# Two spectral layers rewritten around two passes over image planes held with the images innermost

## The chip, the core and the metric

The kernel runs on one core of a Trainium2 chip: PE (TensorE) for matrix products into PSUM banks of 512 float32 columns, DVE (VectorE), ACT (ScalarE) and POOL (GpSimd) for elementwise work, SP and ACT as the issuers of DMAs. The metric is the device time of one execution in microseconds (us). Everything is float32, and each float32 product shows in the trace as two records of PE, each with its weight load; a transpose shows as one.

## The reference

Two layers of the same form act on x of shape (2, 56, 128, 128): two batches of 56 images, 128 by 128. Cut to what matters, one layer is:

```python
def spectral_conv(x, w, b):          # 32 x 16 Fourier modes are kept
    xf = jnp.fft.rfft2(x, norm='forward')
    top = jnp.einsum('bihw,iohw->bohw', xf[:, :, :M1, :M2], _c(w[0]))
    bot = jnp.einsum('bihw,iohw->bohw', xf[:, :, -M1:, :M2], _c(w[1]))
    ...
    return jnp.fft.irfft2(of, s=(H, W), norm='forward') + b

def fno_layer(x, w, b, sw, sb, norm=False, act=False):
    y = spectral_conv(x, w, b)
    if norm: y = inorm(y)
    y = y + skip1x1(x, sw, sb)
    return jax.nn.gelu(y, approximate=False) if act else y

xn = inorm(xa, g1, b1)               # xa: the 112 images
k, q, v = (fno_layer(xn, ...) for each, 8 heads)
scores = jnp.einsum('baks,bals->bakl', qh, kh) * scale
out = softmax(scores) @ v            # mixes the 56 images of a batch
out = fno_layer(out, Pw, Pb, Psw, Psb)
att = inorm(out + xa, gan, ban)
an = inorm(att, g2, b2)
h = fno_layer(an, M0w, ..., norm=True, act=True)
h = fno_layer(h, M1w, ..., norm=True, act=False)
y = inorm(h, gmo, bmo) + att
```

Twice, with weights of their own, `x = x + layer(_gn(x))`, where `_gn` is a group norm over the images of a batch, all h and groups of four w; it has no gain and no offset.

## The kernel before

The planes stand in SBUF as `X` and `A`, each [h, image, w]: 128 partitions of h, 112 images, 128 w. A layer goes over them stage by stage, and each stage goes over all images before the next begins.

- Group norm, then instance norm, for each batch: sums of `X` by products with ones (L340), squares and their sums (L352, L353), the scaling (L364), `bn_stats` of every image row (L326), and the instance norm in place (L376, L378). So the planes are gone over four times on DVE.
- `to_rows` (L270) and `to_modes` (L282, L289) take the planes to 32 x 16 modes, held as `xf` and, with real and imaginary parts exchanged, `xs`. The products of all pairs of images (the Gram matrix) are taken one w at a time (L394), with `A[:, images, w]`, whose elements stand 512 bytes apart, as both operands.
- The scores come from the modes (L386 to L406) and the Gram matrix; softmax; then `D`, the attention applied on the modes (L453 to L455).
- The mix: four w at a time, PE transposes `A` (L462), ACT copies the result to SBUF (L464), PE multiplies with `mix` (L467), and the result goes back into `A`.
- `from_modes` takes modes back to planes: eight small DMAs to memory and two back, a rearrangement on POOL (L308), products L312 and L319. It is used three times in a layer, each with its own finish on DVE: `add_out` (L474, L326), `act` (L542, and ACT's gelu, L545), `skip` (L557, L326). Between these, `to_rows` and `to_modes` are done twice more, and `normed` scales the coefficients.
- The final norm and the sum with the residual (L578 to L582); in the last layer the output DMAs.

The framework places the instructions: the program's order is a first order, and a scheduler moves instructions of each engine within it. The engines then work strictly in the placed order, and tiles of rotating pools set when a buffer comes free.

Of the kernel before, what the change touches and what calls it, by code (L numbers as in the profile page):

```python
# [47 lines left out]
def _constants():  # L48
# [13 lines left out]
    swap[p, p ^ 16] = 1
    row = 8 * (p // 32)[:, None] + np.arange(8)
    edge = kx[:, None] == 0
    sgn = np.where(c == 0, -1.0, 1.0)[:, None]
    own = np.where(edge, 0.5, np.ones((N, 8)))
    mirror = np.where(edge & (row != 16), 0.5, np.zeros((N, 8)))
    count = np.where(edge & (row != 16), 1.0, np.full((N, 8), 2.0))
    count0 = np.where(edge & (row == 0), 0.0, count)
    modes = np.stack([own, mirror, -mirror, count, count * sgn, count0, sgn + np.zeros((N, 8))], 1)  # L70
    place = np.zeros((K, 3 * K))
    place[:, K : 2 * K] = np.eye(K)
# [567 lines left out]
```

## Time and profile before

| what | us |
|---|---|
| three timed runs | 1414.13, 1415.04, 1426.47 |
| their median | 1415.04 |
| profiled execution, span from its first to its last instruction | 1412.7 |
| PE busy in it | 1003.7 |
| DVE busy in it | 819.8 |
| ACT busy in it | 306.0 |
| POOL busy in it | 211.9 |
| mean granted clock of PE | 0.747 |

The span is the only time that is recorded of the profiled execution; the timed runs are other executions. [...] Busy shares are averages over stages that differ, so that a stage is read by its own rows.

### The profile page before, as it was taken

To read this page: it belongs to the slowest core of one execution; us is meant where nothing else is said; L and a number is where in the kernel's file an instruction comes from. 1 tells how busy PE (TensorE), PEld (TensorE's weight loads), DVE (VectorE), ACT (ScalarE), POOL (GpSimd) and SP (SyncE) were. 2 spreads that over 40 slices of the span, in tenths; PEclk is the share of its full clock that TensorE was granted. 3 is DMA by queue.
4 is the path that set the end of the run, shared out by engine and by line. 5 is a ranking of instruction groups with operands and counts; after the bars stand their busy time and mean duration, and the time that the engine had idled before them with its cause. 6 is when DMAs were issued, how large, how long until landed. Compare 5 with 4: busy or idle time off the path is not lost.

```text
span 1412.7 us, 13545 instructions
## 1 busy us (share of the span) xinstructions
PE 1003.7 (71%) x4992; PEld 695.5 (49%) x4992; DVE 819.8 (58%) x2052; ACT 306.0 (22%) x536; POOL 211.9 (15%) x259
## 2 busy tenths in 40 slices
PE   5374899798778936948633849989877887287550
PEld 1151788346664823724212438944566556146320
DVE  2367452791116797528978581739411397873498
ACT  0222200002221203410352321010122112152024
POOL 6603040000001013011131110400000001301102
PEclk9777599665558977979866957986555599599685
DMA  9000000001000010010000000000100000100106
GB/s 260 0 1 1 0 1 1 1 0 26 0 1 1 1 27 0 1 27 1 1 0 1 0 0 1 1 0 0 26 0 1 0 1 0 27 1 1 26 16 193
DMA packets 38872, 22.89 MB, mean 16 GB/s; under 512 B 8606, under 2 KB 37654, under 8 KB 38806
## 3 DMA queue, kind: packets, MB, share of 16 engines
q1 hardware_dynamic: 37216, 20.19, 5.8%
q10 hardware_dynamic: 1590, 1.83, 0.5%
q8 instruction: 39, 0.64, 0.2%
q14 instruction: 27, 0.22, 0.1%
HBM read 11.93 MB, written 10.09 MB: 16 GB/s over the span
## 4 chain that ended last, share of the span: by engine, by line
PE 60%; DVE 22%; ACT 8%; issue 3%; DMA 3%; POOL 3%; SPq 1%; ACTq 0%; POOLq 0%; DVEq 0%
PE mm L270 12%; PE acc L394 9%; PE mm L467 9%; PE mm L319 9%; DVE rows L326 6%; PE mm L453 5%; PE acc L353 3%; PE mm L312 3%; ACT t L464 3%; DVE A L364 2%; DVE A L580 2%; DVE A L557 2%; PE mm L462 2%; PE acc L340 2%; ACT A L128 2%
## 5 line engine op out<-in xcount | busy, mean ns | idle before, releaser
L319 PE MATMUL mm<-c_gw,t 128*128 128x512 f32 x336 | 168.8, 646 | 31.1 <-ACT t L316 31.1
L270 PEld LDWEIGHTS mm<-c_fh,A 128*128 128x128 f32 x1344 | 168.7, 206 | 8.5 <-issue 3.9
L270 PE MATMUL mm<-c_fh,A 128*128 128x64 f32 x1344 | 172.8, 291 | 0.0
L467 PE MATMUL mm<-mixT,t 112*128 112x112 f32 x512 | 131.2, 438 | 46.5 <-ACT t L464 46.5
L467 PEld LDWEIGHTS mm<-mixT,t 112*128 112x128 f32 x512 | 114.1, 328 | 72.8 <-ACT t L464 72.8
L308 POOL COPY lc<-spec 64x128 f32<-64x128 f32 x84 | 52.7, 655 | 627.7 <-PE mm L312 339.0
L126 DVE COPY A<-mm 128x448 f32<-128x448 f32 x32 | 29.1, 908 | 188.2 <-PE mm L467 188.2
L326 DVE BATCH_NORM_STATS2 rows<-A 128x6 f32<-128x128 f32 x672 | 137.0, 275 | 0.1
L394 PE MATMUL acc<-A 128*56 128x56 f32 x1024 | 134.0, 312 | 0.0
L394 PEld LDWEIGHTS acc<-A 128*56 128x56 f32 x1024 | 128.6, 226 | 6.1 <-issue 3.2
L319 PEld LDWEIGHTS mm<-c_gw,t 128*128 128x128 f32 x336 | 65.2, 205 | 108.1 <-issue 52.9
L126 DVE COPY big<-mm 128x512 f32<-128x512 f32 (+1 forms) x50 | 48.2, 971 | 98.6 <-PE mm L270 98.2
L312 PE MATMUL mm<-c_gh,lc 64*64 64x128 f32 x672 | 51.1, 297 | 75.0 <-POOL lc L308 75.0
L128 ACT COPY big<-mm 128x512 f32<-128x512 f32 (+1 forms) x50 | 47.8, 956 | 204.5 <-PE mm L270 138.9
L312 PEld LDWEIGHTS mm<-c_gh,lc 64*64 64x64 f32 x672 | 40.0, 145 | 104.0 <-POOL lc L308 76.1
L353 PE MATMUL acc<-t,ones_gn 128*128 128x512 f32 x112 | 57.1, 665 | 47.6 <-ACT t L352 47.6
L453 PE MATMUL mm<-attnT,big 56*128 56x448 f32 x128 | 82.8, 822 | 3.7 <-DVE spec L454 3.6
L542 DVE SCALAR_TENSOR_TENSOR A<-A,s,mm 128x128 f32<-128x128 f32 x224 | 59.4, 341 | 28.3 <-PE mm L319 28.3
L316 ACT COPY t<-mm 128x512 f32<-128x512 f32 x42 | 24.6, 586 | 220.6 <-PE mm L312 220.6
L462 PE MATMUL mm<-c_ident,A 128*112 128x128 f32 x256 | 68.0, 421 | 0.0
L340 PE MATMUL acc<-X,ones_gn 128*128 128x512 f32 x112 | 60.4, 688 | 10.1 <-DMA X<-x 7.6
L464 ACT COPY t<-mm 112x512 f32<-112x512 f32 x64 | 37.5, 586 | 136.5 <-PE mm L462 136.5
(170 smaller groups left out, 1239.9 us busy)
## 6 DMA issues: line engine op xcount, KB each, us to landing
X<-x SPq DMA_DIRECT2D x14, 512.0 KB, 7.3
out<-X SPq DMA_DIRECT2D x28, 256.0 KB, 2.3
turned<-spec SPq DMA_DIRECT2D x48, 56.0 KB, 2.0
spec<-turned SPq DMA_DIRECT2D x12, 224.0 KB, 3.7
raw<-weights ACTq DMA_DIRECT2D x2, 544.0 KB, 5.0
c_gw<-const_gw ACTq DMA_DIRECT2D x1, 256.0 KB, 5.3
sm<-small ACTq DMA_DIRECT2D x2, 63.0 KB, 5.5
c_swap<-const_swap ACTq DMA_DIRECT2D x1, 64.0 KB, 5.7
```

The source lines that it names most:

```text
L126: nc.vector.tensor_copy(to, of)
L270: nc.tensor.matmul(py[:, 64 * e : 64 * e + 64], lhsT=A[:, i + e, :], rhs=fh, start=True, stop=True)
L312: nc.tensor.matmul(pz[64 * c : 64 * c + 64, N * e : N * e + N], lhsT=four, rhs=gh[:, c, :], start=True, stop=True,)
L319: nc.tensor.matmul(po, lhsT=z[:, N * e : N * e + N], rhs=gw, start=True, stop=True)
L326: nc.vector.bn_stats(rows[:, k, :], A[:, i, :])
L340: nc.tensor.matmul(acc, lhsT=ones_gn, rhs=X[:, i : i + 4, :], start=(i == lo), stop=(i + 4 == hi))
L353: nc.tensor.matmul(acc2, lhsT=ones_gn, rhs=sq, start=(i == lo), stop=(i + 4 == hi))
L394: nc.tensor.matmul(acc[:K, :K], lhsT=plane, rhs=plane, start=(w == 0), stop=(w == N - 1))
L453: nc.tensor.matmul(pv, lhsT=XT[:, b, n, t, :], rhs=aT[b], start=True, stop=True)
L462: nc.tensor.transpose(pt[:I, N * e : N * e + N], A[:, :, w + e], ident)
L464: nc.scalar.copy(xt[:I, :], pt[:I, :])
L467: nc.tensor.matmul(po[:, I * e : I * e + I], lhsT=xt[:I, N * e : N * e + N], rhs=mix, start=True, stop=True)
```

## The change

One layer is written anew. In the code of after:

- The planes stand as `XI` [image, h, w]: 120 partitions, batch 0 in 0 to 55, batch 1 in 64 to 119, zeros between (L164, L165). For the sums over w they are transposed once in a layer into `T` [w, h, image] (L388), with `bn_stats` over the images of four rows at a time (L391), which gives the group norm's mean and variance by a product with `four` (L397, L405).
- `T` is normed in place (L418), and `to_rows` (L304) now takes the sum over w for 16 rows of h, in four products of 32 weight columns, and sends the result by way of memory to `U` [h, mode, image]. The Gram matrix is summed one h at a time, with 64 and 56 weight columns into two halves of one bank (L422). The mean and variance of each image come from the Gram matrix and the modes, so that the instance norm is not applied to the planes at all.
- Scores, softmax and `D` are as before in kind, for both batches in one tile of 120 partitions (L466 to L575).
- The variances that `att`, `an`, M0 and M1 need come from modes, the Gram matrix and the mix `m2` (L585 to L601, L689 to L694), not from planes.
- Pass 1 (L662 to L675) and pass 2 (L722 to L738) are the only two passes over planes after that. `inverse` sums in one bank the modes' contribution (L366, weights of 32 partitions) and the mix of the images (L371, weights from `XI`). Pass 1 applies gelu to it and goes on to the next transform (L304) and the energy of h (L674, L675). Pass 2 scales and adds h (L726 on POOL, L731 on DVE), transposes back (L736) and adds into `XI` (L738). `to_columns` (L341, L352) and `columns` (L357) carry the modes by way of memory to these passes, 480 bytes at a time.
- `prepare` gathers a layer's multipliers in `packed` and reorders them by a product on PE (L272), two copies on ACT and eleven DMAs on SP (L279, L282).

At the head of the program, PE's rows of before and of after (in after `packed` is what POOL makes of the weights; `mm` and `acc` are banks of PSUM, `t2` the squares of `X`, and a number behind a name tells one tile of it from another):

```order
L340 MATMUL acc_202<-X_93,ones_gn_109 128x512 x14
L353 MATMUL acc_221<-t2_223,ones_gn_109 128x512
L353 MATMUL acc_221<-t2_227,ones_gn_109 128x512
L353 MATMUL acc_221<-t2_231,ones_gn_109 128x512
L353 MATMUL acc_221<-t2_235,ones_gn_109 128x512
```

```order
L272 MATMUL mm_219<-c_order_126,packed_178 128x128 [waits DMAHW5_49,Pool_49]
L272 MATMUL mm_219<-c_order_126,packed_178 128x128 [waits Pool_49]
L272 MATMUL mm_219<-c_order_126,packed_178 64x128
L388 MATMUL mm_241<-c_ident_118,XI_93 128x120 [waits DMAHW3_49,DMAHW1_49,DMAHW0_49]
L388 MATMUL mm_241<-c_ident_118,XI_93 128x120 x3
L388 MATMUL mm_249<-c_ident_118,XI_93 128x120 x4
```

The three reordering products, which wait for POOL, now stand ahead of the transposes of the input planes; in before nothing of `prepare` stands on PE.

Where the Gram matrix and the first transform run beside each other, PE's rows of before and of after:

```order
L394 MATMUL acc_846<-A_94 56x56 x16
L270 MATMUL mm_716<-c_fh_121,A_94 128x64 x8
L394 MATMUL acc_846<-A_94 56x56
L270 MATMUL mm_726<-c_fh_121,A_94 128x64 x3
L394 MATMUL acc_846<-A_94 56x56
L270 MATMUL mm_726<-c_fh_121,A_94 128x64 x2
```

```order
L422 MATMUL sums_516<-big_239 64x56
L304 MATMUL mm_519<-big_239,c_fw_122 32x480 x4
L304 MATMUL mm_530<-big_239,c_fw_122 32x480 x4
L422 MATMUL sums_516<-big_239 56x56
L422 MATMUL sums_516<-big_239 64x56
L304 MATMUL mm_541<-big_239,c_fw_122 32x480 x4
L422 MATMUL sums_516<-big_239 56x56
```

In after a Gram product has 64 or 56 weight columns and writes one or the other half of the bank `sums`; `to_rows` has gone from 64 columns for each image to four products of 480.

In the mix of before, and in pass 2 of after, with what each row waits for (`DVE_49` and the like are semaphores):

```order
L462 MATMUL mm_1365<-c_ident_127,A_94 112x128 [waits DVE_49]
L462 MATMUL mm_1365<-c_ident_127,A_94 112x128 x3
L467 MATMUL mm_1372<-mixT_1183,t2_1370 128x112 [waits Activation_49]
L467 MATMUL mm_1372<-mixT_1183,t2_1370 128x112 x3
L462 MATMUL mm_1378<-c_ident_127,A_94 112x128 [waits DVE_49]
L462 MATMUL mm_1378<-c_ident_127,A_94 112x128 x3
L467 MATMUL mm_1385<-mixT_1183,t2_1383 128x112 [waits DVE_49,Activation_49]
L467 MATMUL mm_1385<-mixT_1183,t2_1383 128x112 x3
```

```order
L366 MATMUL mm_1893<-z_1842,basis_894 128x4x56 x2
L371 MATMUL mm_1893<-mixer_1805,XI_93 128x120 x4
L736 MATMUL mm_1902<-c_ident_118,tmp1_160 120x128 [waits DVE_49,PE_49]
L736 MATMUL mm_1902<-c_ident_118,tmp1_160 120x128 x3
L366 MATMUL mm_1911<-z_1908,basis_894 128x4x56 [waits DMAHW4_49,PE_49]
L366 MATMUL mm_1911<-z_1908,basis_894 128x4x56
L371 MATMUL mm_1911<-mixer_1805,XI_93 128x120 x4
L736 MATMUL mm_1920<-c_ident_118,tmp0_158 120x128 [waits DVE_49,PE_49]
```

In both, PE's row of products is followed by one that waits for the engine that takes those products out of PSUM; in after that is the transposes L736 behind L371, with the products of the next quarter behind them.

The diff, cut to its core:

```diff
+        pk = bank()
+        for n in range(3):
+            c = packed[:, 16 * n : min(16 * n + 16, 40), :].rearrange("p n t -> p (n t)")
+            nc.tensor.matmul(pk[: c.shape[1], N * n : N * n + N], lhsT=c, rhs=order, start=True, stop=True)
+        kept = wp.tile([N, 3, N], F32, name="kept")
+        nc.scalar.copy(kept[:, 0:2, :].rearrange("p n m -> p (n m)"), pk[:, 0 : 2 * N])
+        nc.scalar.copy(kept[:64, 2, :], pk[:64, 2 * N : 3 * N])
+        wt = dram.tile([40, 8, N], F32, name="wt")
+        for n in range(3):
+            to = wt[16 * n : min(16 * n + 16, 40)].rearrange("n t m -> (n t) m")
+            nc.sync.dma_start(out=to, in_=kept[: to.shape[0], n, :])
+        mult = wq.tile([N, 40, 8], F32, name="mult")
+        for t in range(8):
+            nc.sync.dma_start(out=mult[t::8], in_=wt[:, t, :].rearrange("n (x s) -> x n s", s=8))
...
-    def to_modes(Y):
+    def to_rows(T, g, turned, U):
+        pv = bank()
+        for q in range(4):
+            nc.tensor.matmul(pv[32 * q : 32 * q + 32, : 4 * J], lhsT=fw, rhs=quarter(T, g, q), start=True, stop=True)
+        v = rows.tile([N, 4, J], F32, name="v")
+        evict(v.rearrange("p i j -> p (i j)"), pv[:, : 4 * J])
+        nc.sync.dma_start(out=by_rows(turned)[g], in_=v)
+        nc.sync.dma_start(out=U[16 * g : 16 * g + 16], in_=turned[16 * g : 16 * g + 16])
...
-    def from_modes(S, use):
+    def columns(turned, g):
+        z = rows.tile([N, 4, J], F32, name="z")
+        nc.sync.dma_start(out=z, in_=by_rows(turned)[g])
+        return z
+
+    def inverse(z, q, basis, mixer, g):
+
+        po = bank()
+        pv = po[:, : 4 * J].rearrange("p (i j) -> p i j", j=J)
+        for b in range(B):
+            cols = slice(R * b, R * b + K)
+            nc.tensor.matmul(
+                pv[:, :, cols], lhsT=basis[32 * q : 32 * q + 32, b, :], rhs=z[32 * q : 32 * q + 32, :, cols],
+                start=(b == 0), stop=False, skip_group_check=True,
+            )
+        for i in range(4):
+            nc.tensor.matmul(
+                po[:, J * i : J * i + J], lhsT=XI[:, 16 * g + 4 * i + q, :], rhs=mixer,
+                start=False, stop=(i == 3), skip_group_check=True,
+            )
+        return pv
...
+        T = big.tile([N, N, J], F32, name="big")
+        stats = st.tile([N, B, 32, 6], F32, name="bn")
+        for h in range(0, N, 4):
+            pt = bank()
             for e in range(4):
-                four = lc[:, 4 * e : 4 * e + 4, :].rearrange("p i k -> p (i k)")
-                for c in range(2):
+                nc.tensor.transpose(pt[:, J * e : J * e + J], XI[:, h + e, :], ident[:J, :J])
+            evict(T[:, h : h + 4, :].rearrange("p h j -> p (h j)"), pt[:, : 4 * J])
+            for b in range(B):
+                nc.vector.bn_stats(stats[:, b, h // 4, :], T[:, h : h + 4, R * b : R * b + K])
...
+        for g in range(8):
+            for b in range(B):
+                v = T[:, 16 * g : 16 * g + 16, R * b : R * b + K]
+                nc.vector.tensor_scalar(v, v, gm[:, b : b + 1], gv[:, b : b + 1], ALU.subtract, ALU.mult)
+            to_rows(T, g, turned, U)
+        for h in range(N):
+            for b, (lo, hi) in enumerate(ROWS):
+                nc.tensor.matmul(
+                    G[lo:hi, :K], lhsT=T[:, h, lo:hi], rhs=T[:, h, R * b : R * b + K],
+                    start=(h == 0), stop=False, skip_group_check=True,
+                )
+        F, Fs = to_modes(U, "F")
...
+        sc = bank()
+        for n, src in enumerate((F, Fs)):
+            for t in range(8):
+                UF = UFs[t]
+                if n and t % 2:
+                    for a in range(HEADS):
+                        nc.scalar.activation(UF[:, a, :], src[:, t, :], AF.Copy, scale=pr["U"][n][:, a, t : t + 1])
+                else:
+                    nc.vector.tensor_tensor(
+                        UF, _bc(src[:, t, :], 1, HEADS), _bc(pr["U"][n][:, :, t], 2, J), ALU.mult
+                    )
+                for b, (lo, hi) in enumerate(ROWS):
                     nc.tensor.matmul(
-                        pz[64 * c : 64 * c + 64, N * e : N * e + N], lhsT=four, rhs=gh[:, c, :], start=True, stop=True,
+                        sc[lo:hi, :AK], lhsT=F[:, t, lo:hi], rhs=UF[:, :, R * b : R * b + K],
+                        start=(n == 0 and t == 0), stop=(n == 1 and t == 7), skip_group_check=True,
                     )
...
+        for g in range(8):
+            z = columns(turned, g)
+            for q in range(4):
+                pv = inverse(z, q, basis, mixer, g)
+                for b in range(B):
+                    cols = slice(R * b, R * b + K)
+                    nc.scalar.activation(quarter(T, g, q)[:, :, cols], pv[:, :, cols], AF.Gelu, scale=gv[:, b : b + 1])
+            to_rows(T, g, turned_h, U)
+            for n in range(2):
+                part = T[:, 16 * g + 8 * n : 16 * g + 8 * n + 8, :]
+                sqh = md.tile([N, 8, J], F32, name="mF")
+                nc.vector.tensor_tensor(sqh, part, part, ALU.mult)
+                nc.vector.tensor_reduce(energy_h[n][:, g, :], sqh.rearrange("p h j -> p j h"), AX.X, ALU.add)
...
-        # A = mix of the images, in place, four w at a time
-        for w in range(0, N, 4):
-            pt = pm.tile([N, 512], F32, name="mm")
-            for e in range(4):
-                nc.tensor.transpose(pt[:I, N * e : N * e + N], A[:, :, w + e], ident)
-            xt = t2.tile([N, 512], F32, name="t2")
-            nc.scalar.copy(xt[:I, :], pt[:I, :])
-            po = pm.tile([N, 512], F32, name="mm")
-            for e in range(4):
-                nc.tensor.matmul(po[:, I * e : I * e + I], lhsT=xt[:I, N * e : N * e + N], rhs=mix, start=True, stop=True)
-            evict(A[:, :, w : w + 4].rearrange("p i w -> p w i"), po[:, : 4 * I].rearrange("p (w i) -> p w i", w=4))
...
+        for g in range(8):
+            z = columns(turned, g)
+            for q in range(4):
+                hc = quarter(T, g, q)
+                nc.gpsimd.tensor_tensor(hc, hc, _bc(c3, 1, 4), ALU.mult)
+                pv = inverse(z, q, basis, mixer, g)
+                tmp = tmps[q % 2]
+                for b in range(B):
+                    cols = slice(R * b, R * b + K)
+                    nc.vector.scalar_tensor_tensor(
+                        tmp[:, :, cols], pv[:, :, cols], gv[:, b : b + 1], hc[:, :, cols], ALU.mult, ALU.add
+                    )
+                pt = bank()
+                for i in range(4):
+                    nc.tensor.transpose(pt[:J, N * i : N * i + N], tmp[:, i, :], ident)
+                xq = XI[:, 16 * g : 16 * g + 16, :].rearrange("p (i q) w -> p q i w", q=4)[:, q]
+                nc.vector.tensor_tensor(xq, xq, pt[:J, :].rearrange("p (i w) -> p i w", w=N), ALU.add)
...
+    layer(*prepare(0), last=False)
     layer(*prepare(1), last=True)
```

## Rows read from the trace of the kernel before

**Rows 1.** The page: its span, and the chain that ended last by engine.

```profile
span 1412.7 us, 13545 instructions
...
PE 60%; DVE 22%; ACT 8%; issue 3%; DMA 3%; POOL 3%; SPq 1%; ACTq 0%; POOLq 0%; DVEq 0%
```

**Rows 2.** Busy time in five stretches of layer 0: us, busy us (x instructions) of each engine, granted clock, DMA.

```profile
0.00:148.00 148.00, 74.57 (x233) 38.59 (x233) 76.89 (x219) 30.28 (x54) 57.57 (x117) 0.79 0.24 62
192.90:240.30 47.40, 47.40 (x384) 47.40 (x384) 26.93 (x18) 0.75 (x2) 19.29 (x8) 1.00 0.00 1
265.50:289.70 24.20, 24.20 (x34) 10.50 (x34) 19.96 (x22) 0.58 (x1) 0.00 (x0) 0.50 0.00 1
314.00:426.00 112.00, 89.92 (x372) 77.28 (x372) 17.75 (x20) 31.17 (x46) 1.52 (x4) 0.50 0.04 9
442.00:470.00 28.00, 24.30 (x124) 11.92 (x123) 27.86 (x103) 2.93 (x5) 2.19 (x6) 1.00 0.00 1
```

**Rows 3.** The chain that ended last, in order of time: start us, us, what.

```profile
240.38 12.03 PE acc L406 x32
...
265.54 24.19 PE mm L453 x32
...
314.08 2.05 PE mm L467 x8
...
580.92 24.97 PE mm L270 x224
```

**Rows 4.** Timeline, the mix of the images, one round of four w.

```profile
332.09 2.05 PE L467 MATMUL mm<-mixT,t 112*128 112x112 f32 x8 [0.73 <-ACT t L464]
...
333.93 1.06 PE L462 MATMUL mm<-c_ident,A 128*112 128x128 f32 x4
...
335.08 0.59 ACT L464 COPY t<-mm 112x512 f32<-112x512 f32 x1
...
335.72 0.56 PE L467 MATMUL mm<-mixT,t 112*128 112x112 f32 x1 [0.73 <-ACT t L464]
```

**Rows 5.** Timeline of PE, products into halves and quarters of the array's columns.

```profile
185.71 1.73 PE L282 MATMUL two<-big,c_fw 128*32 128x448 f32 x16
...
559.01 1.09 PE L312 MATMUL mm<-c_gh,lc 64*64 64x128 f32 x16
```

**Rows 6.** Timeline of PE where two kinds of product alternate.

```profile
155.68 0.48 PE L394 MATMUL acc<-A 128*56 128x56 f32 x2
156.09 1.54 PE L270 MATMUL mm<-c_fh,A 128*128 128x64 f32 x6
157.56 0.48 PE L394 MATMUL acc<-A 128*56 128x56 f32 x2
```

**Rows 7.** Groups by line and shape: busy us, mean ns of one, idle before.

```profile
L326 DVE BATCH_NORM_STATS2 rows<-A 128x6 f32<-128x128 f32 x672 | 137.0, 275 | 0.1
...
L542 DVE SCALAR_TENSOR_TENSOR A<-A,s,mm 128x128 f32<-128x128 f32 x224 | 59.4, 341 | 28.3 <-PE mm L319 28.3
...
L455 DVE TENSOR_REDUCE spec<-spec 128x56 f32<-128x896 f32 x32 | 57.5, 1798 | 0.1
...
L557 DVE SCALAR_TENSOR_TENSOR A<-A,sm,mm 128x512 f32<-128x512 f32 x56 | 39.3, 735 | 31.4 <-PE mm L319 31.4
...
L364 POOL TENSOR_TENSOR A<-A,gvw 128x512 f32<-128x512 f32 x16 | 25.2, 1600 | 45.6 <-DVE gvw L359 45.6
...
L508 DVE TENSOR_TENSOR spec<-spec,m_w 128x896 f32<-128x896 f32 x4 | 4.3, 1082 | 0.0
```

**Rows 8.** Timeline of POOL, the weights of one layer, first and last step.

```profile
14.30 1.33 POOL L172 TENSOR_TENSOR raw<-raw,c_modes 128x544 f32<-128x544 f32 x1
...
28.70 0.45 POOL L232 TENSOR_SCALAR T_im<-T_im,sm 128x64 f32<-128x64 f32 x1
```

**Rows 9.** DMA issues of the page: x count, KB each, median us to landing.

```profile
turned<-spec SPq DMA_DIRECT2D x48, 56.0 KB, 2.0
spec<-turned SPq DMA_DIRECT2D x12, 224.0 KB, 3.7
```

More of the change, by code (lines that the diff above doesn't have):

```diff
@@ L57, in _constants @@
-    for i in range(4):
-        gw[0, i, :, i], gw[1, i, :, i] = cx, -sx
+    twice = np.where(np.arange(16) == 0, 1.0, 2.0)[:, None]
+    gw = np.concatenate([twice * cx, -twice * sx], 0)
+    spare = np.zeros((32, N))
+    spare[16] = 1
     p = np.arange(N)
-    c, kx = p // 16 % 2, p % 16
-    swap = np.zeros((N, N))
[L62 to L72, printed above, removed]
-    arrays = {
-        "fh": fh, "fw": fw, "gh": gh, "gw": gw.reshape(N, 4 * N), "swap": swap,
-        "ident": np.eye(N), "modes": modes, "place": place,
+    kh, c, row = p // 64, p // 32 % 2, p % 32
@@ L76, in _constants @@
+    arrays = {
+        "fw": fw, "fh": fh, "fs": fs, "gh": np.concatenate([gh, gh], 0),
+        "gw": np.stack([np.concatenate([gw] * 4, 0), np.concatenate([spare] * 4, 0)], 1),
+        "swap": swap, "ident": np.eye(N), "modes": modes, "one": one,
+        "wmodes": wmodes, "order": order, "zeros": np.zeros((R - K, 16 * N)),
+        "four": np.kron(np.eye(N // 4), np.full((4, 4), 0.25)),
     }
@@ L282, in to_modes, with to_columns @@
+    def to_columns(S, spare):
+        S1 = relay.tile([N, 32, J], F32, name="relay")
+        turned = dram.tile([N, 32, J], F32, name="turned")
+        for c in range(2):
+            for kh in range(2):
+                for tt in range(2):
+                    p1 = bank()
                     nc.tensor.matmul(
[L283 to L286 removed]
@@ L586, in fno_layers @@
-    first = prepare(0)
-    layer(*first, last=False)
+                        sc[lo:hi, :AK], lhsT=F[:, t, lo:hi], rhs=UF[:, :, R * b : R * b + K],
+                        start=(n == 0 and t == 0), stop=(n == 1 and t == 7), skip_group_check=True,
+                    )
+        nmu = vec("nmu", 1)
+        nc.vector.tensor_scalar(nmu, F[0:1, 0, :], -float(N * N), None, ALU.mult)
+        for b, (lo, hi) in enumerate(ROWS):
+            nc.tensor.matmul(
+                G[lo:hi, :K], lhsT=nmu[:, lo:hi], rhs=F[0:1, 0, R * b : R * b + K],
+                start=False, stop=True, skip_group_check=True,
+            )
@@ new lines, in layer @@
+        Gs = at.tile([J, K], F32, name="Gs")
+        nc.scalar.copy(Gs, G[:J, :K])
+        gd = at.tile([J, K], F32, name="gd")
+        nc.vector.tensor_tensor(gd, G[:J, :K], one[:, :K], ALU.mult)
+        pr_ = bank()
+        nc.vector.memset(pr_[32:64, : K + 1], 0.0)
+        for b, (lo, hi) in enumerate(ROWS):
+            own_ = slice(R * b, R * b + K)
+            nc.tensor.matmul(pr_[lo:hi, :K], lhsT=mean[own_, : hi - lo], rhs=gd[own_], start=True, stop=True)
+            nc.tensor.matmul(pr_[own_, K : K + 1], lhsT=gd[own_], rhs=mean[own_, 0:1], start=True, stop=True)
@@ new lines, in layer @@
+        for b in range(B):
+            own_ = slice(R * b, R * b + K)
+            pt = bank()
+            for a in range(HEADS):
+                nc.tensor.matmul(
+                    pt[own_, K * a : K * a + K], lhsT=s[own_, a, :], rhs=ident[own_, own_], start=True, stop=True
+                )
+            to = aT[own_].rearrange("p a k -> p (a k)")
+            if b:
+                nc.vector.tensor_scalar(to, pt[own_, :AK], r1[own_], None, ALU.mult)
+            else:
+                nc.scalar.activation(to, pt[own_, :AK], AF.Copy, scale=r1[own_])
@@ new lines, in spectral @@
+        def spectral(src, other, n):
+            y = md.tile([N, 8, J], F32, name="y")
+            nc.vector.tensor_tensor(y, src, _bc(pr["M"][:, n, 0, :], 2, J), ALU.mult)
+            for hh in range(2):
+                o = other[hh]
+                half = slice(4 * hh, 4 * hh + 4)
+                t = rows.tile([N, 4, J], F32, name="v")
+                nc.vector.tensor_tensor(t, o, _bc(pr["M"][:, n, 1, half], 2, J), ALU.mult)
+                nc.vector.tensor_tensor(y[:, half, :], y[:, half, :], t, ALU.add)
+            return y
@@ new lines, in layer @@
+        other = []
+        for hh in range(2):
+            po = bank()
+            nc.tensor.matmul(po[:, : 4 * J], lhsT=swap, rhs=Bm[:, 4 * hh : 4 * hh + 4, :], start=True, stop=True)
+            other.append(po[:, : 4 * J].rearrange("p (t j) -> p t j", j=J))
+        y = spectral(Bm, other, 0)
+        q1, al, f, s0, u = (vec(n) for n in ("q1", "al", "f", "s0", "u"))
+        inverse_root(q1, va[:, :J])
+        nc.vector.tensor_scalar(q1, q1, par["gan"], None, ALU.mult)
+        nc.vector.tensor_tensor(u, q1, q1, ALU.mult)
@@ new lines, in layer @@
+        nc.tensor.matmul(pe, lhsT=mean, rhs=eh, start=False, stop=True, skip_group_check=True)
+        nc.tensor.matmul(pm, lhsT=ones[0:1, :], rhs=H[0:1, 0, :], start=False, stop=True, skip_group_check=True)
+        Dq = md.tile([N, 8, J], F32, name="mF")
+        nc.gpsimd.tensor_tensor(Dq, D, _bc(q1, 1, 8), ALU.mult)
+        y = spectral(H, [Hs[:, 0:4, :], Hs[:, 4:8, :]], 1)
+        f1, u, v, a3, c3 = (vec(n) for n in ("f", "u", "al", "a3", "c3"))
+        inverse_root(f1, se)
+        nc.scalar.activation(v, pm, AF.Square)
```

661 lines of the change are left out of this document (326 added, 335 removed).

## The prediction

> **What bounds the kernel now.** I read the page first: PE holds 60% of the chain that ended last and DVE 22% [rows 1], but over stages with different limits, so the stretches come next [rows 2]. In 0 to 148 us (loads, group norm, instance norm) PE and DVE are each busy for half the time; the planes are gone over again and again. In 192.9 to 240.3 PE does nothing but the Gram matrix, 384 passes in 47.40 us at a clock of 1.00. In 265.5 to 289.7 PE is busy throughout at 0.50. The mix, 314 to 426, is also at 0.50, with PE busy for 89.92 of 112 us; and in the last stretch PE (24.30) and DVE (27.86) share 28 us at 1.00. So a stage's price here is its PE passes, times the clock that it gets, plus the waits between engines. The chain gives one stretch of clean passes for each kind [rows 3].
>
> **Prices of a pass.** A float32 product is two passes, a transpose one. With 128 weight columns and 128 or so moving columns: 24.97/224 = 0.11 us at 1.00 [rows 3], 2.05/8 = 0.26 at 0.50 with its first start in it [rows 4]; I take 0.223, twice the former. With 448 moving columns: 12.03/32 = 0.376 at 1.00, 24.19/32 = 0.756 at 0.50 [rows 3]. Into four column quarters 16 passes of 448 take 1.73, 0.11 each, and into two halves 16 of 128 take 1.09, 0.07 [rows 5]. The Gram pass of before costs 47.40/384 = 0.124, more than a plain pass of 128 columns though it moves 56; its operands stand 512 bytes apart. Alternation of two kinds of product: two L394, six L270 and the next two stand 1.88 us apart at starts 155.68, 156.09 and 157.56 [rows 6]; less 2 x 0.124 and 6 x 0.223 that is 0.3 for two changes, 0.15 each. From PE to ACT and back: a round of the mix is 3.63 (332.09 to 335.72 [rows 4]), of which its twelve passes are 2.68; of the 0.95 that is left ACT's copy is 0.59, so the crossing is 0.36.
>
> **Start and weights.** Before, POOL works on one layer's weights from 14.30 to 29.15 [rows 8], beside the loads, and PE doesn't wait for it. In after, three products that need POOL's result stand ahead of the first transpose on PE's row, and the raw weights stand behind eight zero fills and more constants in ACT's DMA queue, while x loads share the engines. Bounds: raw at 14.3 as before, and a start at 31; raw with the last of x, about 34, and a start at 50. I take raw at 30 and the start at **46**, since each DMA of a queue waits for an earlier one of its lane. The second layer's weights are done by then, beside layer 0. After that a layer, in us:
>
> 1. Transposes and `bn_stats`, 32 rounds of four rows of h. PE: four passes, 0.89 at the low clock. DVE: two `bn_stats` of 224 elements at about 0.30 (0.204 for 128, 137.0/672 [rows 7], plus 96 more elements) and every second copy, at 0.65 (ACT's of 512 takes 0.59 [rows 4]): 0.93. 32 x 0.93 = 30. The group statistics, a short chain: 5. This replaces four passes over the planes in 148 us.
> 2. Gram: 256 products, 512 passes. No row shows 56 columns of contiguous operands. Bounds: 0.124 as in the strided case, and 0.055 (a half of 0.11). I take 0.055, as the nearer row is the one into two halves, 0.07 for 128 columns [rows 5]: 28. First transform: 64 passes of 480 in quarters, 7; norm and start 3. Sum 38; the norm of the next rows on DVE lies beside PE.
> 3. Modes and score products: 12 steps on DVE of 960 elements (896 take 1.08 [rows 7], so 1.16), 14, and the transform through memory ahead of it, 8: 22. Softmax: 252.41 to 265.54 is 13.1 [rows 3]; with four more products and their copies, 18. `D`: 265.54 to 314.08 [rows 3], the same DVE reductions of 1.8 us [rows 7], 16 in a layer as before: 48.5, nothing gained.
> 4. Between `D` and pass 1: squares, 33 short products, `spectral` (six DVE steps, 4), a chain of some 14 small steps through ACT and DVE (6), four wide steps (5), eight products with copies (7), a write and a read (2.0 + 3.7 [rows 9]); with waits between engines 38. Between the passes: the same and two transforms: 50. None of this is in the trace; adding the steps alone gives 30 and 40, so 20 less a layer is one end, 20 more the other.
>
> Fixed: 30 + 5 + 38 + 22 + 18 + 48.5 + 38 + 50 = **249** per layer.
>
> **The two passes.** One `inverse` is two products of 224 columns with 32-row weights (0.38 a pass at the low clock, half of 0.756: 1.51) and four of 120 columns (8 x 0.223 = 1.78), and two changes of kind (0.30): 3.59 low, 1.94 at full clock. The copies on ACT (gelu, about 0.35 for 224) and the 480-byte reads of z (224 KB took 3.7 [rows 9]) lie beside groups of 10 us and more; if z came singly after its group, it would cost 8 x 3.7 = 30 a pass.
> - Pass 1, one of eight groups: four inverses, the first transform in quarters (8 passes; 1.85 low, 0.92 full) and the wait for the last gelus (1.1): 17.3 low, 9.8 full; 138 or 78 in all. PE has no wait within a group, but enters from a gap: three groups low and five full, 3 x 17.3 + 5 x 9.8 = 101.
> - Pass 2, one of 32 quarters: the rows of the order show the transposes behind the products that DVE must first scale, and the next inverse behind them. PE waits each time for two DVE steps of 224 (0.265 for 128 and 0.70 for 512 [rows 7], so 0.37 each) and the 0.36 of crossing: 1.1. With four transposes (0.89 low, 0.45 full): 3.59 + 1.1 + 0.89 = 5.58 low, 3.49 full; x32 = 179 or 112. POOL's 32 steps (1600 ns for 512 [rows 7], 1.5 for 480, 48 in all) run ahead. PE would be busy for 80% at the low clock, just the share of the mix [rows 2], which stayed at 0.50 for its 112 us; so I take **179**.
>
> Sum: (249 + 101 + 179) x 2 = 1058, + 46, + 3 for the last output = **1107** of span. The profiled execution of before has a span of 1412.7 and the median of the runs is 1415.04, 2.3 more; so **1110**.
>
> **Rivals.**
> - *The clock rises in pass 2 too.* For: 442 to 470 us, in which PE is busy for 87% and stays at 1.00 [rows 2]. Against: the mix. If it rises after eight of the 32 quarters, pass 2 is 8 x 5.58 + 24 x 3.49 = 129, 50 less a layer: 1010.
> - *Pass 1 stays at the low clock as well.* For: products of few rows, 265.5 to 289.7, always busy and at 0.50 [rows 2]. 138 in place of 101: 1184.
> - *Contiguous operands bring nothing:* a Gram pass stays at 0.124, 512 x 0.069 = 35 a layer: 1180.
> - *Slower than before: changes between 32-row and full-height products stall PE.* There are two a quarter, 64 quarters a layer, 256 in all. It decides from (1412.7 - 1107)/256 = 1.2 us more for each change than my 0.15; at 1.3 more the time is 1443. Against: 0.15 for the alternation in rows 6, but there only the width changes; no row has 32-row weights beside full ones. [...]
>
> **How the numbers follow.** Forecast 0.44; the risen clock 0.30; low in pass 1 0.15; Gram 0.07; stalls 0.04. The low end is the risen clock with 20 less a layer of the fixed parts, 970; the high end pass 1 low with 20 more a layer, 1225. A run of this kernel tells about 1% from no change, 14 us; every case but the last is far beyond it, so faster 0.95, same 0.01, slower 0.04.
>
> **What would show it.** In the page of after PEclk should stand at about 5 through pass 2 and 9 in most of pass 1; a quarter of pass 2 (L366 to L366) at 5.6 us, 3.5 if the clock rose; a group of pass 1 at 10 to 17; L422 at 0.055 a pass; the first L388 at 46; `D` at 48; the gap between the passes at 50. It would be wrong above all through the clock, which alone moves 67 us a layer in pass 2, and through the serial chains of step 4, which I only added up from neighbours.

## The result, and the profile after

The changed kernel takes 1135.54 us (median of 4 runs, 1134.65 to 1142.61) against 1418.4 us of before on the same chip: a ratio of 0.8008, 95% interval [0.7966, 0.8051]. The forecast was 1110 in 970 to 1225. The profiled execution has a span of 1134.5 us where 1107 was forecast.

The page of after, its span, the granted clock in 40 slices, and the chain by engine:

```profile
span 1134.5 us, 10266 instructions
...
PEclk9986886655995755555558888665599685555555
...
PE 58%; DVE 23%; DMA 11%; issue 4%; POOL 1%; ACT 1%; SPq 0%; ACTq 0%; DVEq 0%
```

PE holds 58% of the chain as it held 60% before [rows 1], and DMA now 11%, where it had 3%. The clock's row reads 5 through both passes 2 (slices 15 to 21 and 34 to 40), as forecast. The clock records of the traces of before and of after hold 1.00 and 0.50 alone, and the clock of a stretch is their mean over it. The stretches of layer 0, columns as in [rows 2]:

```profile
0.00:62.90 62.90, 2.14 (x6) 1.29 (x7) 0.33 (x3) 1.28 (x1) 19.38 (x68) 1.00 0.65 154
62.90:95.00 32.10, 20.59 (x130) 18.14 (x130) 29.86 (x82) 10.75 (x19) 13.51 (x40) 0.74 0.12 16
95.00:131.00 36.00, 26.81 (x582) 18.21 (x582) 13.93 (x25) 2.50 (x5) 2.34 (x4) 0.88 0.60 111
131.00:153.60 22.60, 22.60 (x102) 7.80 (x102) 15.45 (x19) 10.37 (x34) 0.00 (x0) 0.88 0.00 1
153.60:170.00 16.40, 8.49 (x76) 7.78 (x77) 9.20 (x19) 4.61 (x8) 0.00 (x0) 0.71 0.00 1
170.00:218.10 48.10, 29.34 (x91) 15.82 (x90) 46.40 (x51) 1.50 (x4) 0.00 (x0) 0.64 0.00 0
218.10:251.40 33.30, 12.99 (x53) 8.39 (x53) 16.56 (x33) 5.45 (x9) 3.16 (x2) 0.65 0.21 74
251.40:362.70 111.30, 104.90 (x448) 69.93 (x448) 46.65 (x34) 28.62 (x69) 0.00 (x0) 0.75 0.20 45
362.70:405.60 42.90, 17.89 (x85) 9.69 (x85) 25.49 (x35) 6.34 (x11) 20.43 (x15) 0.77 0.21 69
405.60:597.30 191.70, 158.10 (x524) 118.93 (x525) 47.91 (x96) 0.58 (x3) 20.91 (x19) 0.50 0.03 8
```

Set beside the terms of the sum:

| stage of layer 0 | forecast | measured |
|---|---|---|
| until the first transpose | 46 | 62.9 |
| transposes, statistics (1) | 35 | 35.9 |
| norm, Gram matrix, first transform (2) | 38 | 32.2 |
| modes and score products (3) | 22 | 22.6 |
| softmax (3) | 18 | 16.4 |
| `D` (3) | 48.5 | 48.1 |
| to pass 1 (4) | 38 | 33.3 |
| pass 1 | 101 | 111.3 |
| between the passes (4) | 50 | 42.9 |
| pass 2 | 179 | 191.7 |

(The second row ends at the first L304, 98.8, the third at 131.0.) Layer 0 sums to 534.4, where 529 was forecast; layer 1 with the last output takes 537.2, where 532 was. The start alone is 16.9 of the 27.5 us by which the forecast was short.

**The start.** POOL's rows between 38 and 50 us:

```profile
38.96 0.20 POOL L218 TENSOR_TENSOR sc<-sm 128x8 f32<-128x8 f32 x1 [35.31 <-DMA sm<-small]
...
44.96 1.33 POOL L205 TENSOR_TENSOR raw<-raw,c_wmodes 128x544 f32<-128x544 f32 x1 [4.56 <-DMA raw<-weights]
...
49.86 1.33 POOL L207 TENSOR_TENSOR raw<-raw 128x544 f32<-128x544 f32 x1
```

The weights land at 44.96, not at 30: their DMA is issued at 30.98 only, behind the zero fills and twelve constants in ACT's queue. The issues wait for earlier DMAs, of SP's queue too: in the chain ACT's constants go on at 27.25, when a load of x lands that was issued at 19.61, and nine of the sixteen loads of x were held up so, for 0.3 to 6.5 us. Then POOL stands for another 1.62 us at the small parameters of the *second* layer, which its row order puts ahead of L207. The first transpose follows at 62.90.

**The Gram matrix and what took its place.** PE at the end of step 2:

```profile
111.98 4.76 PE L422 MATMUL sums<-big 128*56 128x56 f32 x156
...
121.24 3.48 PE L422 MATMUL sums<-big 128*56 128x56 f32 x114 [0.33 <-issue]
130.99 1.07 PE L320 MATMUL mm<-relay,c_fh 128*64 128x480 f32 x2 [6.26 <-issue]
```

156 passes in 4.76 us are 0.0305 each; before it was 47.40/384 = 0.124 [rows 2], and I had taken 0.055. Yet PE then stands for 6.26 us, and the chain there reads `turned<-v` and `relay<-turned`, the transform's way through memory.

**Pass 2**, a quarter:

```profile
405.57 1.83 PE L366 MATMUL mm<-z,basis 32*128 32x224 f32 x4 [8.07 <-DMA z<-turned]
...
407.33 2.06 PE L371 MATMUL mm<-mixer,XI 120*128 120x120 f32 x8
409.50 0.81 DVE L731 SCALAR_TENSOR_TENSOR tmp<-mm,gv,big 128x224 f32<-128x224 f32 x2 [10.82 <-PE mm L371]
...
410.45 1.08 PE L736 MATMUL mm<-c_ident,tmp 128*120 128x128 f32 x4 [1.06 <-DVE tmp L731]
...
411.46 0.74 PE L366 MATMUL mm<-z,basis 32*128 32x224 f32 x1
```

PE's wait for DVE is 1.06 (forecast 1.1). The quarter is 411.46 - 405.57 = 5.89 (forecast 5.58).

**Pass 1**: the transform products of the first two groups, a quarter at full clock, and the last group:

```profile
266.48 1.82 PE L304 MATMUL mm<-big,c_fw 128*32 128x480 f32 x6
...
285.38 1.60 PE L304 MATMUL mm<-big,c_fw 128*32 128x480 f32 x6
286.92 0.64 PE L366 MATMUL mm<-z,basis 32*128 32x224 f32 x2
...
298.02 1.02 PE L366 MATMUL mm<-z,basis 32*128 32x224 f32 x4
...
300.05 1.02 PE L366 MATMUL mm<-z,basis 32*128 32x224 f32 x4
...
344.31 1.83 PE L366 MATMUL mm<-z,basis 32*128 32x224 f32 x4 [5.70 <-DMA z<-turned]
```

A quarter is 2.03 at full clock (forecast 1.94). Before the last group PE waits 5.70 us for z and the clock is down again behind it: two groups at the head and this one run low, five at full clock, as I had split them, but the wait was not in the sum. The clock rises within the L304 products at 285.38, 34 us into the pass. PE is always busy on both sides of that, and the mix of products is the same: from 266.4 to 285.4 at 0.50, with the 32-row products L366 in 7.80 of 19.00 us, and from 286.9 to 338.6 at 1.00, with L366 in 21.43 of 51.70 us.

### The profile page after: what moved, and what is told of

The parts are those of the page before. It is cut to its first block, busy times and chain, and to the rows that moved or that the text cites. A ratio compares the mean times of both kernels' runs of the same rounds, so it can differ in the third digit from the quotient of the medians.

```text
span 1134.5 us, 10266 instructions
## 1 busy us (share of the span) xinstructions
PE 796.8 (70%) x4144; PEld 542.6 (48%) x4144; DVE 503.2 (44%) x782; ACT 140.3 (12%) x314; POOL 126.6 (11%) x186
## 4 chain that ended last, share of the span: by engine, by line
PE 58%; DVE 23%; DMA 11%; issue 4%; POOL 1%; ACT 1%; SPq 0%; ACTq 0%; DVEq 0%
PE mm L371 19%; PE mm L366 17%; PE mm L736 6%; DVE tmp L731 5%; PE mm L304 4%; DVE bn L391 3%; DVE big L570 3%; DVE D L575 3%; DMA turned<-v 3%; PE mm L320 3%; DMA XI<-x 2%; PE mm L472 2%; PE mm L341 2%; DMA z<-turned 2%; DVE big L150 2%
## 5 line engine op out<-in xcount | busy, mean ns | idle before, releaser
L366 PE MATMUL mm<-z,basis 32*128 32x224 f32 x512 | 206.8, 541 | 43.7 <-DMA z<-turned 43.7
L371 PE MATMUL mm<-mixer,XI 120*128 120x120 f32 x1024 | 227.5, 392 | 0.0
L371 PEld LDWEIGHTS mm<-mixer,XI 120*128 120x128 f32 x1024 | 195.4, 285 | 59.0 <-issue 59.0
L366 PEld LDWEIGHTS mm<-z,basis 32*128 32x128 f32 x512 | 127.5, 277 | 105.4 <-issue 93.0
L731 DVE SCALAR_TENSOR_TENSOR tmp<-mm,gv,big 128x224 f32<-128x224 f32 x128 | 51.8, 446 | 216.8 <-PE mm L371 216.8
L736 PE MATMUL mm<-c_ident,tmp 128*120 128x128 f32 x256 | 69.2, 426 | 67.2 <-DVE tmp L731 67.2
L674 DVE TENSOR_TENSOR mF<-big 128x960 f32<-128x960 f32 x32 | 37.1, 1158 | 137.3 <-ACT big L669 136.8
L736 PEld LDWEIGHTS mm<-c_ident,tmp 128*120 128x120 f32 x256 | 45.0, 211 | 83.4 <-issue 83.4
L726 POOL TENSOR_TENSOR big<-big,c 128x480 f32<-128x480 f32 x64 | 78.3, 1260 | 31.1 <-DVE c L711 31.1
L738 DVE TENSOR_TENSOR XI<-XI,mm 120x512 f32<-120x512 f32 x64 | 44.0, 688 | 81.0 <-PE mm L736 81.0
L675 DVE TENSOR_REDUCE F<-mF 128x120 f32<-128x960 f32 x32 | 61.4, 1918 | 0.8
L566 PE MATMUL mm<-aT,big 56*128 56x448 f32 x128 | 47.7, 757 | 17.6 <-DVE big L570 17.4
L304 PE MATMUL mm<-big,c_fw 128*32 128x480 f32 x256 | 56.2, 698 | 0.4 <-DVE big L418 0.4
L575 DVE TENSOR_REDUCE D<-big 128x56 f32<-128x896 f32 x32 | 56.0, 1784 | 0.1
L341 PE MATMUL mm<-y,c_gh 64*128 64x480 f32 x64 | 22.3, 856 | 45.1 <-DVE y L655 25.0
L272 PE MATMUL mm<-c_order,packed 128*128 128x128 f32 (+1 forms) x12 | 3.9, 457 | 60.8 <-POOL packed L252 60.8
L422 PEld LDWEIGHTS sums<-big 128*56 128x56 f32 (+1 forms) x1024 | 31.7, 134 | 20.8 <-issue 17.9
L388 PE MATMUL mm<-c_ident,XI 120*128 120x120 f32 x256 | 36.0, 303 | 7.0 <-ACT big L148 6.8
L391 DVE BATCH_NORM_STATS2 bn<-big 128x6 f32<-128x224 f32 x128 | 40.5, 379 | 0.1
L422 PE MATMUL sums<-big 128*56 128x56 f32 (+1 forms) x1024 | 34.4, 222 | 7.6 <-issue 4.9
```

The lines of the kernel that those rows point to most:

```text
L304: nc.tensor.matmul(pv[32 * q : 32 * q + 32, : 4 * J], lhsT=fw, rhs=quarter(T, g, q), start=True, stop=True)
L366: nc.tensor.matmul(pv[:, :, cols], lhsT=basis[32 * q : 32 * q + 32, b, :], rhs=z[32 * q : 32 * q + 32, :, cols], start=(b == 0), stop=Fals ...
L371: nc.tensor.matmul(po[:, J * i : J * i + J], lhsT=XI[:, 16 * g + 4 * i + q, :], rhs=mixer, start=False, stop=(i == 3), skip_group_check=True,)
L391: nc.vector.bn_stats(stats[:, b, h // 4, :], T[:, h : h + 4, R * b : R * b + K])
L422: nc.tensor.matmul(G[lo:hi, :K], lhsT=T[:, h, lo:hi], rhs=T[:, h, R * b : R * b + K], start=(h == 0), stop=False, skip_group_check=True,)
L566: nc.tensor.matmul(p[:, :AK], lhsT=XT[own_, n, t, :], rhs=aT[own_].rearrange("p a k -> p (a k)"), start=True, stop=True,)
```

## Experiments

Eight tell causes apart, two add what was found. All sit on the changed kernel. "Before" beside them is the kernel before on the same chip.

**1. Full-height basis weights.** Each quarter's 32 rows stand in weights of 128 rows with zeros (`tall`, filled by four copies in a layer).

```diff
-                pv[:, :, cols], lhsT=basis[32 * q : 32 * q + 32, b, :], rhs=z[32 * q : 32 * q + 32, :, cols],
+                pv[:, :, cols], lhsT=tall[:, q, b, :], rhs=z[:, :, cols],
```

> One thing against the changed kernel: the basis products of the inverse take full-height weights, 128 rows with zeros outside the 32 that count, so that no product of 32 rows stands beside full ones in either pass; the count of products and all other work stay. Theory A (in pass 2 PE's wait for DVE holds the clock at 0.50, and a change of product height costs little): a quarter of pass 2 stays between 5.4 and 5.9 us at 0.50, since at most 0.5 of it is changes; time 1085 to 1135. [...]

915.9 us, ratio 0.6462 [0.6433, 0.6491]. That speaks for the other reading, theory B, that the 32-row products hold the clock down: with as many products and the same 1.06 us of waiting, pass 2 rises in its second quarter and stays.

```profile
372.97 1.83 PE L367 MATMUL mm<-z,tall 128*128 128x224 f32 x4 [7.85 <-DMA z<-turned]
...
377.56 1.08 PE L739 MATMUL mm<-c_ident,tmp 128*120 128x128 f32 x4 [1.06 <-DVE tmp L734]
378.43 1.70 PE L367 MATMUL mm<-z,tall 128*128 128x224 f32 x4
...
382.88 0.92 PE L367 MATMUL mm<-z,tall 128*128 128x224 f32 x4
...
385.73 0.62 PE L739 MATMUL mm<-c_ident,tmp 128*120 128x128 f32 x4 [1.05 <-DVE tmp L734]
386.19 0.73 PE L367 MATMUL mm<-z,tall 128*128 128x224 f32 x3
```

A quarter at full clock is 386.19 - 382.88 = 3.31, and pass 2 of layer 0 takes 109.4 us (372.97 to 482.40) where it took 191.7. In pass 1 a quarter at full clock is 1.65 instead of 2.03, two changes of height less: 0.19 each. The first quarter of pass 2, still low, is 5.46 (372.97 to 378.43) instead of 5.89: 0.21 each.

**2. Late transposes.** In pass 2 a quarter's transposes follow the next inverse.

```diff
-                pt = bank()
-                for i in range(4):
-                    nc.tensor.transpose(pt[:J, N * i : N * i + N], tmp[:, i, :], ident)
+                if late:
+                    finish(*late)
+                late = g, q, tmp
```

> One thing against the changed kernel: in pass 2 PE transposes a quarter only after the inverse of the next one, so that it no longer waits for DVE; every product is kept. Theory A: the 1.06 us of waiting go, PE is busy throughout, and the clock rises within the pass as it does in pass 1; a quarter falls from 5.9 to about 2.6, time about 945. Theory B (clock held down by 32-row products): only the wait goes, 4.85 a quarter at 0.50, 64 x 1.06 = 68 less, time about 1067.

1052.99 us, ratio 0.7432 [0.7398, 0.7465]. The wait is gone and the clock stays. PE in pass 2 of layer 0, and one quarter:

```profile
402.90:551.00 148.10, 147.87 (x510) 117.18 (x511) 46.69 (x95) 0.00 (x0) 21.05 (x19) 0.50 0.04 11
```

```profile
415.94 1.86 PE L366 MATMUL mm<-z,basis 32*128 32x224 f32 x4
417.73 2.06 PE L371 MATMUL mm<-mixer,XI 120*128 120x120 f32 x8
419.59 1.06 PE L726 MATMUL mm<-c_ident,tmp 128*120 128x128 f32 x4
420.58 0.74 PE L366 MATMUL mm<-z,basis 32*128 32x224 f32 x1
```

147.87 of 148.10 us busy and 0.50 throughout; a quarter is 4.64. Theory A, that the gap holds the clock down, falls as a sufficient cause. PE was busy, as the profile counts it, for all that time and the granted clock stayed at 0.50, so busy time alone does not decide in this pass.

**3. Filler.** Three products of the mixer's kind on rows that are done, into a bank that nobody reads, between inverse and transposes.

```diff
+                for i in range(3 if g + q else 0):
+                    nc.tensor.matmul(
+                        spare[:, J * i : J * i + J], lhsT=XI[:, done + 4 * i, :], rhs=mixer,
+                        start=True, stop=True, skip_group_check=True,
+                    )
```

> One thing against the changed kernel: in pass 2, three products into a bank that nobody reads are added between the inverse and the transposes of each quarter, work for nothing in the time in which PE waits for DVE. The wait itself is kept. Theory A (the gap holds the clock down): the clock rises, a quarter falls to about 3.6 us although it has three products more, time about 990. Theory B (32-row products hold it down): the clock stays at 0.50, 6 passes of 0.25 replace 1.06 of waiting, 6.35 a quarter, time about 1163.

1002.54 us, ratio 0.7073 [0.7038, 0.7109]: 133 us faster with 186 products more.

```profile
413.44 1.49 PE L731 MATMUL sums<-mixer,XI 120*128 120x120 f32 x6
...
415.35 1.02 PE L366 MATMUL mm<-z,basis 32*128 32x224 f32 x4
...
419.06 0.64 PE L366 MATMUL mm<-z,basis 32*128 32x224 f32 x2
```

The clock rises in the second quarter and is 0.96 over 403.90 to 530.00; a quarter is then 419.06 - 415.35 = 3.71. As theory A had it in time; but run 2 shows that closing the gap is not enough. What this run has and run 2 lacks is more full-height work beside the same 32-row products.

**4. Weights of 64 rows**, half of them zeros, in place of run 1's 128.

```diff
-                pv[:, :, cols], lhsT=tall[:, q, b, :], rhs=z[:, :, cols],
+                pv[:, :, cols], lhsT=tall[64 * (q // 2) : 64 * (q // 2) + 64, q, b, :], rhs=z[64 * (q // 2) : 64 * (q // 2) + 64, :, cols],
```

> As the run with full-height basis weights, but the weights take 64 rows (32 that count and 32 of zeros), so that products of another height still stand beside full ones. If only the change of height kept the clock down, pass 2 stays at 0.50 with a quarter of 5.9 us, and the time is about 1135. If it goes by how many rows the products work on, 64 rows may be enough or not: if they are, pass 2 stands at 1.00 with a quarter of 3.31 + 0.25 for two changes = 3.56, and the time is about 916 + 128 x 0.25 = 948; if they are not, 1135 again.

1123.82 us, ratio 0.7896 [0.7843, 0.795].

```profile
401.50:590.00 188.50, 154.85 (x514) 116.41 (x512) 47.75 (x96) 0.00 (x0) 19.68 (x18) 0.50 0.03 8
```

Low through pass 2. It leaves two readings: the height changes here too. Pass 1 does answer to the 64 rows: its clock rises about 19 us into the pass instead of 34, within the first group's transform products (both layers), and in run 1 with 128 rows about 5 us in.

**5. A tiny 32-row product** of 8 columns in each quarter of run 1, so that the height changes as often as in the changed kernel.

```diff
+        o = 32 * ((q + 1) % 4)
+        nc.tensor.matmul(
+            pv[:, 0, 0:8], lhsT=tall[o : o + 32, q, 0, :], rhs=z[o : o + 32, 0, 0:8],
+            start=False, stop=False, skip_group_check=True,
+        )
```

> The run with full-height basis weights, with one product of 32-row weights over 8 columns put between the basis and the mixer products of every quarter (it adds zeros), so that the height changes twice a quarter as in the changed kernel, while nearly all of PE's work stays at full height. If the changes of height keep the clock at 0.50, pass 2 goes back to 0.50 and a quarter to 5.9 us, time about 1140. If it is that a third of PE's time goes into products of few rows, pass 2 stays at 1.00 with two changes of 0.13 and two short passes more, 3.31 + 0.4 = 3.7, and pass 1 pays the same: 128 x 0.4 = 51 over the run without the tiny products, about 967.

1042.84 us (1033.54 to 1065.13), ratio 0.7292 [0.724, 0.7343]: neither of the two forecasts. Most of pass 2 of layer 0, and 120 us of that of layer 1:

```profile
392.00:516.00 124.00, 90.59 (x547) 75.49 (x547) 44.95 (x90) 0.00 (x0) 22.90 (x20) 0.93 0.07 16
...
880.00:1000.00 120.00, 99.73 (x355) 81.96 (x355) 29.12 (x58) 0.00 (x0) 2.33 (x3) 0.50 0.18 49
```

Layer 0 rises in the third quarter, layer 1 only in the 23rd (at 1000 us), with the same instructions. So with the changes in it pass 2 had 0.93 over 124.00 us in one layer and 0.50 over 120.00 us in the other: the changes do not keep the clock at 0.50 by themselves, and with the gap beside them the rise came at two different moments.

**6. The tiny product and late transposes together:** no gap, changes as in run 2, few-row work small.

> Full-height basis weights, the tiny 32-row product in every quarter, and late transposes in pass 2: PE has no wait in pass 2, as in the run with late transposes alone, and changes height twice a quarter, as there, but few-row work is a small part of its time instead of a third. If the changes of height keep the clock down, pass 2 stays at 0.50 as there, with about 5.0 us a quarter: 837 + 64 x 2.9 = 1023 or more. If the share of few-row work does, the clock rises within the first quarters of each pass 2 and stays: 2.1 + 0.5 = 2.6 a quarter, 837 + 128 x 0.45 = 895.

920.17 us, ratio 0.6466 [0.6425, 0.6506]. Both layers rise in the third quarter and stay; both passes 2, and one quarter:

```profile
391.00:480.00 89.00, 88.28 (x574) 77.49 (x575) 44.10 (x95) 0.00 (x0) 20.94 (x19) 0.93 0.07 18
817.00:905.00 88.00, 87.41 (x567) 76.83 (x568) 42.99 (x92) 0.00 (x0) 21.53 (x19) 0.93 0.33 93
```

```profile
403.83 0.92 PE L367 MATMUL mm<-z,tall 128*128 128x224 f32 x4
404.69 0.38 PE L372 MATMUL mm<-z,tall 32*128 32x8 f32 x2
...
406.43 0.73 PE L367 MATMUL mm<-z,tall 128*128 128x224 f32 x3
```

A quarter is 2.60. Run 2 had the same number of changes and no gap; what differs is that the basis products work on 128 rows and the 32-row work is small, 0.5 of 4.9 us at the low clock against 1.79 of 4.64 there. So it was the 32-row basis products, not the changes of height, that kept pass 2 of run 2 at 0.50: 0.50 over 148.10 us there, 0.93 over 89.00 and 88.00 here. Their share alone is no rule: in pass 1 of the changed kernel it is as large (7.80 of 19.00 us), and that pass rises.

**7. The head of the queue.** Small parameters, layer 0's weights and three constants first among ACT's DMAs.

```diff
+    sms = [parts(0), parts(1)]
+    raw0 = raws(0)
+    wmodes, order, ident = load("wmodes"), load("order"), load("ident")
     XI = planes.tile([J, N, N], F32, name="XI")
```

> One thing against the changed kernel: the small parameters of both layers, layer 0's raw weights and the two constants that POOL and the reordering need are issued first in ACT's DMA queue, ahead of the zero fills. Theory A (the first transposes wait for POOL's work on the weights, whose DMAs stand late in the queue): the first transpose moves from 63 us to about 30 and the group statistics from 95 to about 60, bounded then by the loads of x; time about 1100. Rival (the loads bound the start anyway, whatever the order in the queue): the statistics end no earlier than 85 us, time 1125 or more.

1103.6 us, ratio 0.779 [0.7748, 0.7832]. The first transpose stands at 27.29, 35.6 us earlier, and its stage lasts a little longer than the 32.10 of the changed kernel, with one wait of 2.52 us for x in it:

```profile
27.30:60.80 33.50, 18.77 (x129) 16.85 (x128) 30.32 (x82) 11.22 (x20) 11.11 (x31) 0.88 0.64 139
```

**8. The Gram matrix twice**, the second time into a bank that nobody reads.

```diff
+        again = bank()
+        for h in range(N):
+            for b, (lo, hi) in enumerate(ROWS):
+                nc.tensor.matmul(
+                    again[lo:hi, :K], lhsT=T[:, h, lo:hi], rhs=T[:, h, R * b : R * b + K],
+                    start=(h == 0), stop=(h == N - 1), skip_group_check=True,
+                )
```

> The changed kernel with the 256 products of the Gram matrix done a second time in each layer, into a bank that nobody reads. By the prediction's price of 0.055 a pass and PE as what bounds there, 512 x 0.055 = 28 a layer, time 1192. By the spacing in the trace of after (0.0305) and the 6.3 us for which PE waits there for the transform's DMAs, 15.6 - 6.3 = 9.3 a layer, time 1154; if the DMAs alone bound the stage, less than 5 more.

1159.06 us, ratio 0.8134 [0.809, 0.8179], on a chip whose before took 1426.39; the span is 1154.3, 19.8 over after's. From the first L304 (97.03) to the second transform (141.81) it is 44.8 in layer 0, where it was 32.2:

```profile
131.03 10.89 PE L429 MATMUL mm<-big 128*56 128x56 f32 x369 [1.15 <-issue]
...
141.81 0.57 PE L320 MATMUL mm<-relay,c_fh 128*64 128x480 f32 x1
```

So a Gram matrix more costs 10 to 13 us of its 15.6: the rest fits into the 6.26 us in which PE stood. PE and the DMAs both bound this stage, within about 6 us of each other.

**9. Full-height weights and late transposes**, both edits as above.

> Full-height basis weights and, in pass 2, the transposes of a quarter behind the next inverse. If the two gains are of different kinds (the clock, and PE's wait for DVE of 1.05 us), they add: 64 x 1.05 = 67 below the run with full-height weights, about 848, with a quarter of pass 2 at 2.26. Rival: DVE (0.81 + 0.69 and its own crossings, some 1.9 us a quarter) or the reuse of the two tmp tiles takes over, and a quarter stays at 2.6 or more: 870 or more.

837.21 us, ratio 0.5875 [0.5846, 0.5905]. They add: 79 us less than run 1, where late transposes alone took 83 off the changed kernel. A quarter of pass 2 is 383.32 - 381.24 = 2.08, where 2.26 was expected.

**10. All of it**, with three buffers for z.

```diff
-        z = rows.tile([N, 4, J], F32, name="z")
+        z = rows.tile([N, 4, J], F32, name="z", bufs=3)
```

> Full-height basis weights, late transposes in pass 2, the weights' DMAs at the head of the queue, and three buffers in place of two for the columns z. If the gains add: 848 less 32 for the start, less about 5 a layer for the wait of the last group's z in pass 1: about 806. If the z load still stands behind a row of v on its queue, about 816.

789.98 us, ratio 0.5545 [0.5518, 0.5572], 346 us below the changed kernel. The wait for z inside pass 1 is gone; pass 1 and pass 2 of layer 0 now:

```profile
219.60:300.00 80.40, 73.31 (x450) 57.58 (x451) 53.08 (x37) 28.62 (x69) 0.00 (x0) 0.95 0.29 69
336.70:410.00 73.30, 72.67 (x545) 71.96 (x546) 46.67 (x101) 2.08 (x5) 21.02 (x19) 0.97 0.09 23
```

## Why the prediction was right, and where its working was not

- **Clock of pass 2.** 0.50 was right, the reason was not, so that the choice of 179 over 112 came out by luck. I read it off the mix: busy for 80% and low [rows 2]. Run 2 is busy for all of pass 2 and low; run 1 has the gap and rises. The nearer row was the other one, 265.5 to 289.7 [rows 2]: 56-row products, always busy, 0.50, with no change of kind. I used it only for the rival in pass 1, and at 0.15. The rival that the clock rises by itself had 0.30 on the same wrong ground; with the basis in 32 rows and no full-height work added, pass 2 of the changed kernel (0.50 over 191.70 us in layer 0 and 193.60 in layer 1) and of run 2 (0.50 over 148.10) did not rise. Nor does the row of 56-row products give a rule: behind 16 full-height transposes the clock rises, and seven of the same products take 0.46 each where they took 0.756:

```profile
289.66 3.64 PE L446 MATMUL mm<-c_ident,spec 128*56 128x128 f32 x16
293.23 3.23 PE L453 MATMUL mm<-attnT,big 56*128 56x448 f32 x7
```

- **Pass 1.** The split of three low and five full groups was an estimate with no row behind it and held by luck: the start of a pass was low for two, and the third was low behind the wait for z. That the reads of z "lie beside groups of 10 us and more" failed once a layer: z of the last group stands behind a row of `turned<-v` in SP's queue, 5.70 of the 10.3 us by which the pass was short. Run 10 removes it.
- **Change of height.** 0.15 was taken from rows 6, where only width changes. It measures 0.19 at full clock and 0.21 at the low one (run 1). That is far from the 1.2 us from which the slower case would have decided; what PE does in a change, no run shows. Two changes, and four transposes at 1.01 instead of 0.89 (410.45 to 411.46), make most of the 0.31 by which a quarter of pass 2 was short; 32 of them are 10 of the 12.7 us.
- **Gram.** Mis-sized: 0.0305 a pass, not 0.055, and so 15.6 instead of 28; step 2 came out 5.8 short of the forecast, not 12.4, because the transform's DMAs then bound (run 8).
- **Start.** 46 lay within bounds of 31 and 50, and 62.9 came. Issues did wait for earlier DMAs, as the choice of 46 had it (nine of sixteen loads of x); the step that failed is "raw at 30": I took the weights as landing at 30, when their DMA is only issued at 30.98 and takes 14 us more; the upper bound, the last of x, counted no queueing behind it. I also did not see that POOL's row waits for the second layer's parameters as well. Run 7 confirms the rest: POOL's work follows the landing, and the stage after it is DVE's 30 us.
- **`D`** was right, 48.1 for 48.5, and the short chains of step 4 took 76 for 88. So the sum came near because errors cancelled: in layer 0 the two passes took 23.0 more than forecast and the fixed parts 17.6 less. DVE's 48 us for `D` are now the longest stage of a layer beside the two passes.

What pass 1 has and pass 2 lacks is a row of full-height transform products in each group. In pass 1 with the basis in 32 rows (the changed kernel and runs 2, 3 and 7, both layers) PE is low up to the first six transform products behind the second group, which start 34.0 to 34.1 us into the pass, and the clock rises within them, or less than 1 us behind them; with 128 rows and no tiny product (runs 1, 9 and 10, both layers) it rises in the second quarter, about 5 us in, ahead of any. No run took these products out of pass 1, so that they raise the clock is not shown.

What stays open: why the clock rises at the second group's row and not at the first one's, and why run 5, with the gap, rose in the third quarter once and in the 23rd the other time, where run 6, without it, rose in the third both times. The mix of before, without products of so few rows but with PE idle for 22.08 of its 112.00 us [rows 2], stayed at 0.50. Whether gaps count beside rows, and how the two add up, no run here separates.

## What to carry to other kernels

Read the granted clock beside what the products look like, not beside the busy share alone: pass 2 was busy for 147.87 of 148.10 us at 0.50 (run 2), and with full-height weights its quarter went from 4.64 to 2.08 (run 9); zeros that fill 32 rows to 128 cost no pass more and here bought 220 us (run 1). A rewrite that strips one engine's work shows the next order of limits (a wait between engines in each small step, the first loads, a queue's order), and a few lines each took them off: 79 and 32 us here, and 15 as what is left of run 10's gain. When a term is taken at full clock or low, say by which row, and look whether another row speaks for the other reason.
